# The order of side pieces in an attention stage: turned maxima first, one normalisation a step, the second half of a list later

## The chip, the cores and the metric

The kernel runs on one core of a Trainium2 chip. Its time is device time in microseconds (us) for one execution; the median of the runs is compared. The engines are TensorE (PE; its weight loads are PEld), VectorE (DVE), ScalarE (ACT), GpSimd (POOL) and SyncE (SP), which here only issues DMAs.

## What is computed

Four sequences of 512 tokens with 256 features go through two residual blocks, all in float32. The reference, cut to its core:

```python
# block 1: x = x + attn(cond_mlp(x, cond_8))
expert = jnp.argmax(opcode_onehot, axis=-1)            # one expert of 8 for a sequence
hidden = jax.nn.silu(up) * gate                        # 256 -> 512
out    = einsum('bsh,bdh->bsd', hidden, wd) + bd       # 512 -> 256
q = (einsum('bte,oe->bto', x, Wq) + bq) * scaling      # 16 heads of 16
k, v = kv[..., :16], kv[..., 16:]                      # one key and value head for all
attn_probs = softmax(einsum('brd,bsd->brs', qr, k))    # 16 x 512 query rows, 512 keys
out = einsum('bte,oe->bto', attn_output, Wo) + bo
# block 2: x = x + ffn(cond2(x, cond_8))
w_bot = einsum('bg,got->bot', y, weight * mask)        # a mixed 256 x 256 matrix per sequence
x2 = einsum('bnt,bot->bno', x, w_bot) + bias
probs = softmax(einsum('gth,he->gte', xg, w_router))   # 8 experts, 8 groups of 256 tokens
_, idx = top_k(probs, 2)                               # places by cumsum, at most 128 per group and expert
h = gelu(einsum('gech,ehf->gecf', expert_in, wi)); expert_out = einsum('gecf,efh->gech', h, wo)
out = einsum('gech,gtec->gth', expert_out, combine)
```

## The kernel before

**Stages.** First (to about 110 us) the sequences' gated layers, with the first projection. Then attention in 64 steps, with everything that a finished sequence needs next to it (output projection, mixing, routing, and the scatter of its rows to a table `xp` in DRAM that is ordered by expert). Last, from about 381 us, the expert layers: units of 256 or 128 rows of `xp` that have one expert, with 2 MB of weights for each. Every engine executes its instructions in the order in which the kernel is written: the schedule is by hand, and the lists `beside`, `last` and `final` name the side pieces of each step.

**A step.** The loop at the end of the function runs over n = 0 to 64. The step n belongs to sequence b = n // 16, with k = n % 16. It makes
- `maxima(m, ...)` for m = n + 6 (LEAD): four matmuls of scores (L375) and four reductions on VectorE (L379) that give the negated row maxima of 4 x 128 query rows in the tile `negm`;
- `exponentials(n, ...)`: four matmuls (L404) of the transposed scores of a group of 128 x 16 query rows with 128 keys, and four exponentials on ScalarE (L408);
- `weigh(n - 1, ...)`: eight products with the values (L422, 16 matmuls in the profile) into the one PSUM bank `a`; after the fourth step of a group the bank is copied to `stage` (L431: by ScalarE, in the last two groups by VectorE) and written to `od` in DRAM (L432);
- `side(b, k)`: the pieces that the lists name for this k. An entry (-1, "norm0") is piece norm0 of the sequence one back; (1, "q0") of the next; (0, ...) of the same.

The scores' matmuls write three PSUM banks `m`; the first two of each four exponentials, and the pieces, four banks `x`. In a plain step the order is: two maxima, two exponentials, half of weigh, two maxima, two exponentials, the side pieces, the other half of weigh. In a dense step, one whose pieces have large matmuls (the names in ON_PE), the pieces stand in the middle and weigh comes whole at the end. From n = 58 there are no maxima left, and a step has exponentials, weigh and side pieces.

**A group's turn.** After four steps of maxima (m % 4 == 3, so n % 4 == 1) `shifted(m // 4)` turns the group's 128 x 128 of `negm` (L387, VectorE) and writes it by four small DMAs on SP (L391) into the odd rows of the query tile. The exponentials of that group begin three steps later, and their matmuls subtract the maxima.

```python
        if m < STEPS and m % 4 == 3:
            shifted(m // 4)
```

stands at the end of the step, behind the side pieces.

**The pieces that matter here**, by their lines: `bias` adds a vector to a sequence's input rows x on VectorE (L493; x is read by `residual`, L301, into the one buffer x that the last sequence must have left); `inv` and `norm0`, `norm1` make the reciprocal of the softmax sums (L472, with a way through DRAM, L473 and L477) and multiply two halves of the attention result by it (L485); `out0` to `out3` project it (L502 on TensorE), add it to x (L507) and write the rows out (L508, SP); `rT` transposes x (L523, copied by ScalarE, L524); `mix` multiplies by the mixed matrix (L534, L538); `choose`, `rank0`, `rank1` find the two experts of each token (L551 to L582; one exponential on ScalarE between, L554); `places` counts (L600 on TensorE), `rows` and `send` compute the rows in `xp` (L613 to L649, the last being `to_i`), and `row0` to `row3` scatter (L655, eight indirect DMAs by POOL).

**The list of first units.** During the last sequence (list `last`) the first six expert units are already chosen from the first sequences' counts: `pairs0` (k = 3) starts a list of two, `pairs1` (k = 8) ends it (L840 to L876 on VectorE, fourteen small instructions) and issues on SP the fetch of the first unit's weights wi (L907; SP loads its row from the table first, L914) and of the rows xt of units 0 and 1 (L929); `pairs2` (k = 12) lists four more; `pairs3` (k = 13) fetches more weights and transposes unit 0's rows on TensorE (`turn(0)`, L971, copied by L973); `pairs4` (k = 15) fetches more weights. The rows of unit 2 are fetched first thing in the expert stage, when the scatters so far have landed, and `turn(2)` follows unit 1's first layer (L1035).

Of the kernel before, what the change touches and what calls it, by code (L numbers as in the profile page):

```python
# [42 lines left out]
def adaln_attn_ffn_kernel(  # L43
# [32 lines left out]
    def bank(tag):  # L76
        return ps.tile([P, 512], F32, tag=tag, name=f"ps_{tag}", bufs=BANKS[tag])
# [220 lines left out]
    def residual(b):  # L298

        t = rp.tile([P, 4, D], F32, name="x", bufs=1)  # L300
        nc.sync.dma_start(t, xtok[:, ts(b, 4), :])  # L301
        seqs[b]["x"] = t

    def project(b):

        s = seqs[b]
        s["q"] = q_tiles[b % 2]

        def queries(co):
            def piece():  # L310
                pq = bank("x")
                for c in range(2):
                    mm(pq, wq_sb[:, c, ts(co, P)], coT[:, c, ts(b, T)], start=c == 0, stop=c == 1)  # L313
                qs = qp.tile([P, T], F32, name="stage", bufs=4)
                nc.scalar.activation(
                    qs, pq, AF.Identity, bias=bqs_sb[:, co : co + 1], scale=HD**-0.5
                )
                for n in range(2):
                    nc.sync.dma_start(qd[co, 0:P:2, n, :], qs[ts(n, 64), :])
                nc.sync.dma_start(s["q"][:, ts(co, 2), :], qd[co])  # L320
            return piece

        def keys():

            s["k"] = qp.tile([P, T], F32, name="k")
            pk = bank("x")
            for c in range(2):
                mm(pk, wk_sb[:, c, :], coT[:, c, ts(b, T)], start=c == 0, stop=c == 1)  # L328
            nc.scalar.activation(s["k"], pk, AF.Identity, bias=bk_sb)

        def values():
            s["v"] = v_tiles[b % 2]
            pv = bank("x")
            for sc in range(4):
                nc.tensor.transpose(pv[:, ts(sc, P)], s["k"][:, ts(sc, P)], ident)
            nc.vector.tensor_copy(
                s["v"][:, :, 0:HD].rearrange("p s (j d) -> p s j d", j=2),
                pv.rearrange("p (s j d) -> p s j d", s=4, j=4)[:, :, 0:2, 3:19:2],
            )

        return {
            "q0": queries(0), "q1": queries(1), "k": keys, "v": values,
        }
# [39 lines left out]
    def shifted(u):  # L383

        b, hg = divmod(u, 4)
        nmT = qp.tile([P, 4, 32], F32, name="nmT")
        nc.vector.transpose(  # L387
            nmT.rearrange("p i t -> p (i t)"), negm[u % 2].rearrange("p i j -> p (i j)")
        )
        for a in range(4):  # L390
            nc.sync.dma_start(  # L391
                seqs[b]["q"][1:P:32, :, ds(hg * P + 32 * a, 32)],
                nmT[32 * a : 32 * a + 4],
            )

    def exponentials(n, js):
        u, sc = divmod(n, 4)
        k = seqs[u // 4]["k"]
        if n not in e_of:
            e_of[n] = ep.tile([P, 4, 4, P], F32, name="e")  # L400
        for n4, j in enumerate(js):
            px = bank("m" if n4 >= 2 else "x")
            rows_j = slice(32 * j, 32 * j + 32)
            mm(  # L404
                px, k[rows_j, ts(sc, P)], seqs[u // 4]["q"][rows_j, :, ts(u % 4, P)],
                start=True, stop=True,
            )
            nc.scalar.activation(  # L408
                e_of[n][:, :, j, :].rearrange("p h (i t) -> p i h t", i=4),
                px.rearrange("p (i h t) -> p i h t", i=4, h=4), AF.Exp,  # L410
            )
# [287 lines left out]
    def route_mixed(b):  # L699
# [25 lines left out]
        [(-1, "values"), (1, "k"), (-2, "places"), (-2, "rows")],  # L725
        [(-2, "send")],
        [(-1, "inv"), (-2, "row0")],
        [(-2, "row1")],
        [(-1, "norm0"), (-1, "norm1"), (-2, "row2")],
        [(-1, "out0"), (-1, "out1"), (-2, "row3")],  # L730
        [(-1, "out2"), (-1, "out3")],
        [(-1, "rT0"), (-1, "rT1"), (1, "v")],
        [(-1, "mix0"), (-1, "mix1")],
        [(-1, "mix2"), (-1, "mix3")],
        [],
        [(-1, "choose")],
        [(0, "bias")],
        [],
    ]
    last = [  # L740
# [1 line left out]
        [(-2, "rank1")],  # L742
        [(-1, "values"), (-2, "places"), (-2, "rows")],
        [(-1, "inv"), (0, "pairs0")],
        [(-2, "send"), (-2, "row0")],
        [(-1, "norm0"), (-1, "norm1"), (-2, "row1")],
        [(-1, "out0"), (-1, "out1"), (-1, "out2"), (-1, "out3"), (-2, "row2")],
        [(-1, "rT0"), (-1, "rT1"), (-2, "row3")],
        [(-1, "mix0"), (-1, "mix1"), (-1, "mix2"), (-1, "mix3"), (0, "pairs1")],
        [(-1, "choose"), (-1, "rank0")],  # L750
        [(-1, "rank1")],
        [(-1, "places"), (-1, "rows"), (-1, "send"), (-1, "row0")],
        [(0, "values0"), (0, "pairs2"), (-1, "row1")],
        [(0, "pairs3"), (-1, "row2")],
# [12 lines left out]
    STEPS = 16 * B  # L767
    work = {b: finish(b) for b in range(B)}

    def side(b, k):  # L770

        for off, name in (last if b == B - 1 else beside)[k]:
            to = b + off
            if not 0 <= to < B:
                continue
            if name[:5] == "pairs":
                first_pairs(name[5:])
                continue
            if off == 1:
                if name == "q0":  # L780
                    projection[to] = project(to)
                projection[to][name]()
            else:
                work[to][name]()
# [157 lines left out]
    def first_pairs(part):  # L942
        if part == "0":
            parts.append(list_of_pairs(0, N0))
            next(parts[0])
        elif part == "1":
            next(parts[0], None)
            fetch_in(0)
            fetch_rows(0)
            fetch_rows(1)  # L950
        elif part == "2":
            for _ in list_of_pairs(N0, NA - N0):
                pass
        elif part == "3":

            i = fetch_in(1)
            tc.add_manual_dep(i.ins, weighed[-1].ins.name, AFTER, reason="not at once")
            fetch_out(0)
            turn(0, "x")
        else:  # L960
            i = fetch_in(2)
            tc.add_manual_dep(i.ins, weighed[-1].ins.name, AFTER, reason="not at once")
            fetch_out(1)
# [56 lines left out]
    def up(u, half):  # L1020

        if is_small(u):
            if half == 0:
                up_small(u)
            return
        n = width(u) * P
        if half == 0:
            t = ep.tile([P, 4, 4, P], F32, name="e").rearrange("p a b t -> p (a b t)")
            hT_of[u] = t[:, 0 : F // P * n].rearrange("p (f t) -> p f t", f=F // P)
        each = 512 // n  # L1030
        for f0 in range(4 * half, 4 * half + 4, each):
            ph = bank("m")
            for k in range(each):
                for c in range(2):
                    mm(  # L1035
                        ph[:, ts(k, n)], wi_of[u][:, c, ts(f0 + k, P)], xT_of[u][:, c, :],
                        start=c == 0, stop=c == 1,
                    )
            nc.scalar.activation(  # L1039
                hT_of[u][:, f0 : f0 + each].rearrange("p f t -> p (f t)"), ph,  # L1040
                AF.Gelu_apprx_tanh,
            )
# [63 lines left out]

    for n in range(STEPS + 1):
        m = n + LEAD
        if n in (0, 26, 42, 56):
            residual((0, 26, 42, 56).index(n))  # L1110
        b, k = divmod(n, 16)
        names = [name for _, name in (last if b == B - 1 else beside)[k]] if b < B else []
        dense = any(
            name.rstrip("0123") in ON_PE and (b > 0 or name in projection[0]) for name in names
        )
        if m >= STEPS:
            if n < STEPS:
                exponentials(n, (0, 1, 2, 3))
            if n == STEPS:

                up(0, 0)
            weigh(n - 1, (2, 3))
            weigh(n - 1, (0, 1))
            if n < STEPS:
                side(b, k)
        elif dense:

            maxima(m, (0, 1))
            exponentials(n, (2, 3))
            side(b, k)  # L1130
            maxima(m, (2, 3))
            exponentials(n, (0, 1))
            if n > 0:
                weigh(n - 1, (2, 3))
                weigh(n - 1, (0, 1))
        else:

            maxima(m, (0, 1))
            exponentials(n, (2, 3))
            if n > 0:  # L1140
                weigh(n - 1, (2, 3))
            maxima(m, (2, 3))
            exponentials(n, (0, 1))
            side(b, k)
            if n > 0:
                weigh(n - 1, (0, 1))
        if m < STEPS and m % 4 == 3:
            shifted(m // 4)

    places = itertools.count()  # L1150

# [157 lines left out]
```

## Time and profile before

| | |
|---|---|
| median of 3 runs | 654.48 us (654.36 to 656.58) |
| the profiled execution | 652.61 us |
| its span, first to last instruction | 650.9 us |
| mean granted TensorE clock | 0.989 |
| TensorE busy (matmul) | 630.8 us, 97% of the span |
| VectorE, ScalarE, POOL busy | 330.4, 225.1, 111.9 us |
| L379, 250 reductions of 128x512 | 684 ns each |
| L408, 244 exponentials of 128x512 | 594 ns each |
| L493, a bias | 1.22 us |
| L387, a turn | 0.29 to 0.31 us |

The share of busy time is a mean over stages. The attention stage (about 112 to 381 us) has VectorE at half to nine tenths and DMA queues mostly idle; the expert stage has little VectorE work and DMA engines at eight to nine tenths. Matmuls are pipelined and their ends are modelled, so a TensorE that is held up for a short time can still look busy; the lengths of the steps show it better. A line of a timeline has the start, the duration, engine, line, operation, tiles and count, and in brackets how long the engine had been idle and what ended that. A row of the table of windows has a stretch, its length, the busy time of PE, PEld, DVE, ACT and POOL (with instructions), the granted clock, the share of DMA time and GB/s.

### The profile page before, as it was taken

The numbers are of one execution on the slowest core, as the hardware profiler recorded it, in microseconds if no ns is written. First come the engines' busy times: TensorE is split into PE (matmuls) and PEld (weight loads), VectorE is DVE, ScalarE is ACT, GpSimd is POOL, SyncE is SP. The second block draws the span as 40 slices with busy tenths as digits, with TensorE's granted clock in tenths as the row PEclk, the third lists the DMA queues.
The fourth block names the chain that finished last, engine by engine and source line by source line (L and its number), as shares of the span: only waits on it lengthen the run. The fifth ranks groups of instructions, "written<-read, shape, count | busy, mean of one in ns | idle before, by whom it ended". The sixth has DMA issues, their size and how long they took to land.

```text
span 650.9 us, 10666 instructions
## 1 busy us (share of the span) xinstructions
PE 630.8 (97%) x4004; PEld 373.9 (57%) x4004; DVE 330.4 (51%) x810; ACT 225.1 (35%) x400; POOL 111.9 (17%) x146
## 2 busy tenths in 40 slices
PE   9999999999999999999999899999999999999991
PEld 3444454333334433343335368888899999777781
DVE  1184745577767687867896653357122221232320
ACT  1112123566664565545554551221111112012210
POOL 1600000000000000500022141216422222312332
PEclk9999999999999999999999899999999999999996
DMA  7953981300132104411033399636899999888611
GB/s 234 360 160 90 306 250 34 98 18 34 21 130 84 51 18 117 142 58 49 19 103 116 125 318 309 210 96 207 253 268 320 322 337 298 266 259 274 193 18 23
DMA packets 65469, 107.20 MB, mean 165 GB/s; under 512 B 6915, under 2 KB 27011, under 8 KB 65411
## 3 DMA queue, kind: packets, MB, share of 16 engines
q1 hardware_dynamic: 50066, 87.96, 41.4%
q0 software_dynamic: 6464, 8.79, 6.8%
q10 hardware_dynamic: 8880, 9.71, 4.8%
q8 instruction: 33, 0.54, 0.3%
q14 instruction: 26, 0.20, 0.1%
HBM read 79.59 MB, written 26.71 MB: 163 GB/s over the span
## 4 chain that ended last, share of the span: by engine, by line
PE 87%; DMA 6%; DVE 3%; issue 1%; POOL 1%; SPq 0%; ACT 0%; POOLq 0%
PE ps_m L375 19%; PE ps_x L1068 15%; PE ps_m L1035 15%; PE ps_a L422 9%; PE ps_a L279 4%; PE ps_x L263 4%; PE ps_x L281 4%; PE ps_x L534 2%; PE ps_x L313 2%; PE ps_x L404 2%; PE ps_x L502 2%; DMA wo_sb<-in_wo_dram 2%; DMA inv<-ivd 2%; DMA inv<-od 1%; PE ps_x L1005 1%; PE ps_x L328 1%
## 5 line engine op out<-in xcount | busy, mean ns | idle before, releaser
L379 DVE TENSOR_REDUCE negm<-ps_m 128x1 f32<-128x512 f32 x250 | 160.5, 684 | 65.0 <-PE ps_x L404 46.2
L408 ACT ACTIVATE e<-ps_x 128x512 f32<-128x512 f32 x244 | 132.4, 594 | 108.5 <-PE ps_x L404 101.4
L375 PE MATMUL ps_m<-k,q 32*128 32x512 f32 x500 | 152.3, 639 | 0.4 <-DVE negm L379 0.4
L404 PE MATMUL ps_x<-q,k 32*128 32x512 f32 x488 | 139.7, 642 | 1.9 <-DMA q<-nmT 1.9
L1035 PE MATMUL ps_m<-xT,wi_sb 128*128 128x256 f32 (+1 forms) x672 | 115.4, 330 | 0.0
L1068 PE MATMUL ps_x<-wo_sb,e 128*128 128x256 f32 x512 | 114.3, 379 | 0.0
L1035 PEld LDWEIGHTS ps_m<-xT,wi_sb 128*128 128x128 f32 x672 | 103.7, 191 | 9.7 <-issue 0.4
L1068 PEld LDWEIGHTS ps_x<-wo_sb,e 128*128 128x128 f32 x512 | 95.6, 190 | 12.6 <-issue 0.4
L1039 ACT ACTIVATE e<-ps_m 128x512 f32<-128x512 f32 x64 | 38.0, 597 | 175.6 <-PE ps_m L1035 174.0
L375 PEld LDWEIGHTS ps_m<-k,q 32*128 32x128 f32 x500 | 46.5, 183 | 55.7 <-DVE negm L379 25.9
L422 PE MATMUL ps_a<-e,v 128*32 128x256 f32 x1024 | 76.6, 392 | 0.1
L1082 POOL DMA_INDIRECT out_dram<-y,to_row x36 | 55.7, 1548 | 122.2 <-DMA out_dram<-y,to_row 32.0
L422 PEld LDWEIGHTS ps_a<-e,v 128*32 128x32 f32 x1024 | 23.3, 109 | 80.2 <-issue 67.3
L973 DVE COPY xT<-ps_a 128x256 f32<-128x256 f32 (+1 forms) x23 | 12.2, 528 | 84.4 <-PE ps_a L971 84.4
L1078 DVE TENSOR_SCALAR y<-ps_x,w 128x256 f32<-128x256 f32 x32 | 15.4, 482 | 63.9 <-PE ps_x L1068 63.9
L655 POOL DMA_INDIRECT xp<-x,to_i x32 | 33.6, 1051 | 53.8 <-DVE negm L379 28.8
L404 PEld LDWEIGHTS ps_x<-q,k 32*128 32x128 f32 x488 | 38.2, 184 | 4.4 <-issue 4.2
L584 POOL TENSOR_SCALAR x<-mk 128x4 f32<-128x4 f32 x4 | 0.8, 211 | 208.2 <-DVE mk L581 208.1
L284 DVE SCALAR_TENSOR_TENSOR hid<-ps_x,wo_sb,sg 128x512 f32<-128x512 f32 x16 | 12.0, 749 | 45.2 <-PE ps_x L281 45.2
L279 PE MATMUL ps_a<-xT_sb,wi_sb 128*128 128x512 f32 x64 | 30.5, 599 | 0.1
L281 PE MATMUL ps_x<-xT_sb,wi_sb 128*128 128x512 f32 x64 | 30.1, 592 | 0.0
L263 PE MATMUL ps_x<-hid,wo_sb 128*128 128x512 f32 x64 | 28.8, 597 | 0.0
(165 smaller groups left out, 464.7 us busy)
## 6 DMA issues: line engine op xcount, KB each, us to landing
wi_sb<-in_wi_dram SPq DMA_DIRECT2D x25, 1024.0 KB
wo_sb<-in_wo_dram SPq DMA_DIRECT2D x25, 1024.0 KB
xp<-zeros ACTq DMA_DIRECT2D x1, 8712.0 KB
q<-qd SPq DMA_DIRECT2D x8, 512.0 KB
wi_sb<-in_wcond_dram SPq DMA_DIRECT2D x15, 256.0 KB
od<-stage SPq DMA_DIRECT2D x15, 256.0 KB
xt<-xp SPq DMA_DIRECT2D x11, 264.0 KB
wo_sb<-in_wcond_dram SPq DMA_DIRECT2D x4, 517.0 KB
```

The source lines that it names most:

```text
L263: mm(po, wd[:, hc, ts(dc, P)], hid_of[b][:, hc, :], start=hc == 0, stop=hc == 3)
L279: mm(pu, wu[:, c, :], xT_sb[:, c, ts(b, T)], start=c == 0, stop=c == 1)
L281: mm(pg, wg[:, c, :], xT_sb[:, c, ts(b, T)], start=c == 0, stop=c == 1)
L375: mm(pm, q[32 * j : 32 * j + 32, i, ts(hg, P)], k[32 * j : 32 * j + 32, :], start=True, stop=True,)
L379: nc.vector.tensor_reduce(nm[:, i, j : j + 1], pm, AX.X, ALU.max, negate=True)
L404: mm(px, k[rows_j, ts(sc, P)], seqs[u // 4]["q"][rows_j, :, ts(u % 4, P)], start=True, stop=True,)
L408: nc.scalar.activation(e_of[n][:, :, j, :].rearrange("p h (i t) -> p i h t", i=4), px.rearrange("p (i h t) -> p i h t", i=4, h=4), AF.Exp,)
L422: i = mm(pa_of[u][32 * hh : 32 * hh + 32, j0 * P : (j0 + nj) * P], seqs[b]["v"][:, sc, :], e[:, hh, j0 : j0 + nj].rearrange("p j n -> p (j ...
L1035: mm(ph[:, ts(k, n)], wi_of[u][:, c, ts(f0 + k, P)], xT_of[u][:, c, :], start=c == 0, stop=c == 1,)
L1039: nc.scalar.activation(hT_of[u][:, f0 : f0 + each].rearrange("p f t -> p (f t)"), ph, AF.Gelu_apprx_tanh,)
L1068: mm(po[:, 0:D], hT_of[u][:, fc, ts(h, P)], wo_of[u][:, fc, :], start=fc == 0, stop=fc == F // P - 1,)
L1082: i = nc.gpsimd.indirect_dma_start(out=out_rows, out_offset=bass.IndirectOffsetOnAxis(ap=to, axis=0), in_=y, in_offset=None, compute_op=AL ...
```

## The change

`shifted` moves from the end of the step to the place behind the last exponentials: in a plain step ahead of the side pieces, in a dense one ahead of weigh. In `beside` (sequences 0 to 2) the bias of a sequence moves from k = 14 of its own steps to k = 5 of the next sequence's; `norm0` and `norm1` are parted to k = 6 and 7; the output pieces, transposes, mixes and the values of the next sequence (`v`) move one step back, to k = 8 to 12; `choose` stays at 13. In `last` (the steps of sequence 3) the bias of sequence 2 comes at k = 4, ahead of the send of sequence 1; `pairs1` moves from k = 8 to k = 10, behind the second rank, where no maxima are left; the last sequence's own bias stays at k = 14. The reading of x for sequences 1 and 2 moves from n = 26 and 42 to 27 and 43. The number of instructions stays the same.

```diff
     beside = [
...
         [(-1, "inv"), (-2, "row0")],
-        [(-2, "row1")],
-        [(-1, "norm0"), (-1, "norm1"), (-2, "row2")],
-        [(-1, "out0"), (-1, "out1"), (-2, "row3")],
+        [(-1, "bias"), (-2, "row1")],
+        [(-1, "norm0"), (-2, "row2")],
+        [(-1, "norm1"), (-2, "row3")],
+        [(-1, "out0"), (-1, "out1")],
         [(-1, "out2"), (-1, "out3")],
         [(-1, "rT0"), (-1, "rT1"), (1, "v")],
         [(-1, "mix0"), (-1, "mix1")],
         [(-1, "mix2"), (-1, "mix3")],
+        [(-1, "choose")],
         [],
-        [(-1, "choose")],
-        [(0, "bias")],
         [],
     ]
     last = [
...
         [(-1, "inv"), (0, "pairs0")],
-        [(-2, "send"), (-2, "row0")],
+        [(-1, "bias"), (-2, "send"), (-2, "row0")],
...
-        [(-1, "mix0"), (-1, "mix1"), (-1, "mix2"), (-1, "mix3"), (0, "pairs1")],
+        [(-1, "mix0"), (-1, "mix1"), (-1, "mix2"), (-1, "mix3")],
         [(-1, "choose"), (-1, "rank0")],
-        [(-1, "rank1")],
+        [(-1, "rank1"), (0, "pairs1")],
...
-        if n in (0, 26, 42, 56):
-            residual((0, 26, 42, 56).index(n))
+        if n in (0, 27, 43, 56):
+            residual((0, 27, 43, 56).index(n))
...
             side(b, k)
             maxima(m, (2, 3))
             exponentials(n, (0, 1))
+            if m % 4 == 3:
+                shifted(m // 4)
...
             maxima(m, (2, 3))
             exponentials(n, (0, 1))
+            if m % 4 == 3:
+                shifted(m // 4)
             side(b, k)
...
-        if m < STEPS and m % 4 == 3:
-            shifted(m // 4)
```

## The prediction, made before the changed kernel was run

> **What bounds the kernel now.** I read the page, then a table of windows cut at the ends of the steps, then the end of the attention stage engine by engine.
>
> The page, parts 1 and 2: TensorE works nearly all the time, so only stretches in which it waits can be won, and one slice of the clock row (the 23rd, 358 to 374 us) is below full speed.
> ```profile
> PE 630.8 (97%) x4004; PEld 373.9 (57%) x4004; DVE 330.4 (51%) x810; ACT 225.1 (35%) x400; POOL 111.9 (17%) x146
> PEclk9999999999999999999999899999999999999996
> ```
> Windows; a row is a stretch, its length, each engine's busy time, granted clock, DMA share:
> ```profile
> 221.71:226.83 5.12, 5.12 (x44) 2.48 (x44) 3.35 (x7) 2.17 (x5) 0.00 (x0) 1.00 0.19 70
> 226.83:230.36 3.53, 3.53 (x36) 1.19 (x36) 2.36 (x5) 1.77 (x5) 0.00 (x0) 1.00 0.00 0
> 237.44:241.52 4.08, 4.08 (x37) 1.34 (x36) 4.08 (x6) 2.18 (x6) 0.00 (x0) 1.00 0.01 1
> 200.31:206.52 6.21, 5.61 (x44) 2.64 (x44) 5.37 (x10) 2.58 (x6) 0.00 (x0) 1.00 0.20 69
> 272.38:279.11 6.73, 5.48 (x44) 2.50 (x44) 5.38 (x9) 2.56 (x6) 3.18 (x3) 1.00 0.45 161
> 357.38:362.15 4.77, 4.39 (x36) 1.23 (x35) 3.71 (x10) 2.22 (x5) 0.00 (x0) 1.00 0.64 195
> 367.11:373.09 5.98, 4.07 (x32) 1.45 (x32) 2.88 (x18) 2.44 (x6) 1.05 (x1) 0.75 0.02 4
> ```
> In order: a step with matmuls of side pieces (5.12); a plain one (3.53); the one after a bias (4.08, VectorE busy throughout); the ones after a pair of normalisations, sequences 1 and 2 (6.21, 6.73, against 5.12); step 57, behind the list's second half (4.77); step 60, which waits and then runs at 0.75 clock. Its cause, in the timeline of TensorE, VectorE and SP:
> ```profile
> 357.86 0.42 SPq L907 DMA_DIRECT2D wi_sb<-in_wi_dram  x1
> 361.60 1.29 DVE L379 TENSOR_REDUCE negm<-ps_m 128x1 f32<-128x512 f32 x2 [0.94 <-PE ps_x L404]
> 365.16 0.30 DVE L387 STREAM_TRANSPOSE nmT<-negm 128x128 f32<-128x128 f32 x1
> 367.31 0.39 PE L600 MATMUL ps_x<-hot,ones 128*128 128x64 f32 x2
> 369.61 0.74 PE L404 MATMUL ps_x<-q,k 32*128 32x512 f32 x2 [1.91 <-DMA q<-nmT]
> 370.86 0.17 DVE L649 TENSOR_TENSOR to_i<-pos,to 128x8 int32<-128x8 f32 x1
> 373.16 0.69 DVE L431 COPY stage<-ps_a 128x512 f32<-128x512 f32 x1 [2.13 <-PE ps_a L422]
> 375.33 0.66 PE L971 MATMUL ps_x<-ident,xt 128*128 128x128 f32 x4
> 387.94 0.38 SPq L929 DMA_DIRECT2D xt<-xp  x1
> 396.11 0.57 PEld L971 LDWEIGHTS ps_a<-ident,xt 128*128 128x128 f32 x4
> ```
> The last maxima are reduced at 362.89, but turned only at 365.46, behind the router's choice; TensorE gets them 4.15 later.
>
> **Part A, pieces in steps 0 to 56.** A bias keeps VectorE for 1.14 us (237.94 to the next reduction at 239.08), and the step after it is 0.55 longer: 0.59 of a piece is absorbed. Before: three biases, 0.64, 0.54, 0.55 (steps of 4.18, 4.07, 4.08); two pairs of normalisations, 6.21 − 5.12 = 1.09 and 6.73 − 5.12 = 1.61; together 4.43. After, in sequences 1 and 2: the bias stands behind the turn (0.31) of the same step, 1.14 + 0.31 − 0.59 = 0.86; the first normalisation (0.95, half of the pair's 1.89) 0.95 − 0.59 = 0.36; the second ends 0.95 after its reductions, while TensorE wants it for out0's second product some 0.75 after them, 0.2: 1.42, twice 2.84. The last sequence's step 4 gets a bias ahead of the send; there VectorE runs without a break from 316.85 (DVE-bound steps of 3.7 to 4.6), so the bias costs its whole 1.14. The turn ahead of both its normalisations delays them by 0.3, which the 0.31 idle found before 337.24 pays. After 3.98, gain **0.45**. Ends: with nothing absorbed beyond the 0.45 that VectorE idles per half step, seven pieces cost 0.14 more each, a loss of 0.5; with normalisations free, a gain of 1.55. I take the middle rows, as the bias is the nearest piece.
> The four output pieces, the two transposes and the mixes move a step later, with their out_dram DMAs on SP and copies on ACT; five such steps stay five, and SP waits there for adds that are due anyway: 0, and 0.3 an output piece (its add is 0.42) if not. Reading x at 27 and 43 moves with the transposes; its reader is ten steps off. The turns of k 1 and 13 change places with a piece of their own step: 0, at most the 0.31 of one turn.
>
> **Part B, the list's second half leaves step 56.** VectorE is freed of 355.70 to 358.15 (2.45); step 57 becomes plain, 4.77 − 3.54: gain 1.23. On SP the weight fetch and two row fetches (357.86 to 360.97) go behind the four turn DMAs.
>
> **Part C, the last turn.** Reductions now end at 362.89 − 1.23 = 361.66, the turn at 361.97, its data reaches TensorE 4.15 later, 366.12. TensorE comes at 367.69 (end of L600) − 1.23 = 366.46: the wait goes. Step 60 lasts 2.31 (the plain tail step 373.09 to 375.40) and not 373.09 − 367.69 = 5.40: gain 3.09, of it 1.91 waiting and 1.18 half clock. B and C promise 4.32.
>
> **Part D, what is late next.** VectorE's queue behind the turn: choice and first rank 2.43 (362.81 to 365.24), second rank 1.26, now the list 2.45, then rows and send 3.31 (367.73 to 371.04), and only then L431's copy (0.69), which empties the one bank that step 61's weighing writes: 361.97 + 2.43 + 1.26 + 2.45 + 3.31 + 0.69 = 372.11. TensorE is there at 366.46 + 2.31 + 1.31 (the exponentials' products) = 370.08: it waits 2.1. Weighing ends at 373.17; then it wants turn(0)'s rows. The trace's DMA records have them landed at 364.21, 8.51 after the list began; the list now begins at 365.66, so 374.17: another 1.0. The transposes end at 374.83, before at 375.99: of 4.32, **1.16** is left.
> Then turn(2), at 396.11. Its rows (issued 387.94, when the last of eight scatters had landed) are complete at 396.00 in the DMA records: TensorE had 0.1 us to spare. They hang on to_i, at 371.04 before and 371.42 after, and on queue q1, which serves wi and xt until 374.5 and then the rest, which in before began at 374.71. So they land no earlier, TensorE waits some 1.05 there, and **0.1** is kept. Ends: 1.16 kept, if the landing moves with TensorE; a loss of 0.3, if it follows to_i.
> The waits of 2.1 and 1.0 may bring the half clock back. The trace: after 1.91 us without work the clock was 0.75 over step 60, costing 1.18; by that row the same again is lost, and the 1.05 of waiting at turn(2) takes it in but for 0.1.
> [...]
>
> **The sum.** 0.45 + 0.1 − 0.1 ≈ 0.45. The profiled execution took 652.61 (span 650.9 and 1.7 around it): 652.15 after. The runs' median, 654.48, lies 1.9 above it; the same change gives **654.0**. A measurement of this kernel tells about 0.5% (3.3 us) from no change.
>
> **Rivals.**
> *Kept as far as turn(0)* (19%): landings move with TensorE. For it: scatters and fetches follow the same step. Against: their source, to_i, does not move. 654.48 − 0.45 − 1.16 = 652.9.
> *All kept* (13%): if choice, ranks and list leave the copy and turn(0) no later than TensorE wants them. For it: VectorE is 49% idle over the span. Against: the 10.1 us of queue counted in D. 654.48 − 0.45 − 4.32 = 649.7; with half of D's waits, 651.5.
> *The fetches push the DMA queue* (11%): the moved fetch's packets (358.95 to 364.53, 5.58 us, in a stretch otherwise idle) now end where the crowded stretch starts; a window from 374 to 640 us has a DMA share of 0.80. If they delay all behind them by X, turn(2) passes on all but 0.1. From X = 0.6 it is slower than before, from X = 3.9 by over 0.5%; with all 5.58: 654.48 − 0.45 + 5.58 − 0.1 = 659.5. Against: the sum has them done 0.2 before that stretch.
> *VectorE's pieces cost more* (7%): A at its bad end, no half clock hidden: 654.48 + 0.5 + 1.1 = 656.1.
> The forecast itself has 50%, with 653.2 to 655.0. Faster by over 0.5% (below 651.2) is most of *all kept*, 12%; slower (above 657.8) most of the queue's, 10%; within, 78%. The range, 651.8 (A's best end and 1.16 kept) to 656.4 (A's bad end, 0.3 lost at turn(2), and a half clock not hidden), leaves out some 2 in 10.
>
> **What would show it.** Step 57 at 3.5; no wait for q<-nmT at step 60; TensorE waiting at L422 for the copy of L431, then at L971 for xt; the copy straight after to_i; a half clock around 372 to 377; turn(2) with a wait. Steps of about 4.4 after the bias, of 3.9 and 5.3 with the normalisations, 1.1 more at the last sequence's step 5. Wrong would be a tail in which VectorE has idle time before L431, or rows of turn(2) that come a microsecond earlier.

## The result, and the profile after

| | changed | before |
|---|---|---|
| median of 12 runs each, side by side | 654.04 | 655.14 |
| lowest to highest | 652.75 to 656.07 | 653.78 to 656.63 |
| profiled execution (span) | 653.83 (652.0) | 652.61 (650.9) |
| step 56 ends at | 357.69 | 357.38 |
| step 64 ends at | 386.75 | 385.53 |

The ratio is 0.9993, with a 95% interval of 0.9981 to 1.0006: no difference that can be measured. The quotient of the two medians, 0.9983, lies in that interval too. The profiled execution of the changed kernel is typical of its runs; that of the kernel before was 2.5 below the median of the 23 runs that came with the first experiments (655.15). A second profile of the kernel before, told below, took 654.56.

Three lines of the page of the changed kernel, of busy times, clock and costliest groups:

```profile
PE 633.2 (97%) x4004; PEld 375.6 (58%) x4004; DVE 331.1 (51%) x810; ACT 225.0 (35%) x400; POOL 111.4 (17%) x146
...
PEclk9999999999999999999999989999999999999997
...
L422 PE MATMUL ps_a<-e,v 128*32 128x256 f32 x1024 | 76.6, 392 | 1.4 <-DVE cmp L823 1.3
```

TensorE's busy time grew by 2.4 (630.8 before) with as many matmuls: some of them ran at half clock, in a later slice than before. And L422 now has idle time in front of it, 1.4, released by VectorE.

Windows cut at the ends of steps 22, 23, 24, 53, 55, 57, 61 and 62, with the columns as in the prediction:

```profile
196.41:200.91 4.50, 4.50 (x37) 1.44 (x36) 4.45 (x8) 2.18 (x6) 0.00 (x0) 1.00 0.52 173
200.91:204.45 3.54, 3.54 (x34) 1.20 (x34) 3.19 (x6) 2.17 (x6) 0.00 (x0) 1.00 0.02 4
204.45:209.72 5.27, 5.27 (x44) 2.68 (x44) 4.26 (x8) 2.56 (x6) 0.00 (x0) 1.00 0.16 53
332.86:337.69 4.83, 4.46 (x37) 1.22 (x36) 4.68 (x12) 2.65 (x7) 1.04 (x1) 1.00 0.47 165
345.38:350.79 5.41, 5.41 (x45) 2.47 (x44) 3.85 (x6) 4.22 (x8) 1.96 (x2) 1.00 0.42 130
357.69:361.23 3.54, 3.54 (x37) 1.20 (x36) 2.41 (x5) 2.26 (x6) 0.00 (x0) 1.00 0.20 74
...
368.90:373.14 4.24, 2.90 (x25) 1.03 (x24) 3.79 (x22) 3.21 (x7) 0.94 (x1) 1.00 0.92 320
373.14:379.29 6.15, 5.00 (x31) 1.90 (x31) 3.82 (x15) 1.19 (x2) 4.79 (x5) 0.50 0.89 256
```

The reader is to see: the step behind a bias (4.50), behind the first normalisation (3.54, as if nothing were there) and behind the second (5.27); the bias in the last sequence (4.83); step 57 without the list (3.54). Then what came instead: step 61, with 1.34 without a matmul, and step 62, all of it at a clock of 0.50.

The timeline of the end, lines of VectorE and TensorE:

```profile
361.74 0.31 DVE L387 STREAM_TRANSPOSE nmT<-negm 128x128 f32<-128x128 f32 x1
...
371.15 0.17 DVE L649 TENSOR_TENSOR to_i<-pos,to 128x8 int32<-128x8 f32 x1
...
371.24 0.68 DVE L431 COPY stage<-ps_a 128x512 f32<-128x512 f32 x1
...
372.07 1.07 PE L422 MATMUL ps_a<-e,v 128*32 128x256 f32 x16 [1.34 <-DVE cmp L823]
...
374.29 1.12 PE L971 MATMUL ps_x<-ident,xt 128*128 128x128 f32 x4 [1.15 <-DMA xt<-xp]
...
397.53 0.60 PE L971 MATMUL ps_a<-ident,xt 128*128 128x128 f32 x4
```

The last turn comes 3.42 earlier than before (365.16), and no wait for q is left. L422 starts right behind the copy L431, which stands in VectorE's queue behind the choice, the list and the send (the profile names the small instruction that ends 0.05 before it). Then TensorE waits for the first unit's rows. The clock was half from 373.18 to 380.01, 6.83, against 3.41 before.

### The profile page after: what moved, and what is told of

It reads as the page before. It is cut to its first block, busy times and chain, and to the rows that moved or that the text cites. A ratio compares the mean times of both kernels' runs of the same rounds, so it can differ in the third digit from the quotient of the medians.

```text
span 652.0 us, 10666 instructions
## 1 busy us (share of the span) xinstructions
PE 633.2 (97%) x4004; PEld 375.6 (58%) x4004; DVE 331.1 (51%) x810; ACT 225.0 (35%) x400; POOL 111.4 (17%) x146
## 4 chain that ended last, share of the span: by engine, by line
PE 92%; DVE 3%; DMA 2%; issue 1%; POOL 1%; SPq 0%; ACT 0%; POOLq 0%; DVEq 0%
PE ps_m L375 20%; PE ps_m L1035 17%; PE ps_x L1068 16%; PE ps_a L422 10%; PE ps_a L279 4%; PE ps_x L263 4%; PE ps_x L281 4%; PE ps_x L534 2%; PE ps_x L313 2%; PE ps_x L502 2%; PE ps_x L404 2%; PE ps_a L971 1%; PE ps_x L1005 1%; PE ps_x L328 1%; PE ps_m L985 1%; DVE negm L379 1%
## 5 line engine op out<-in xcount | busy, mean ns | idle before, releaser
L422 PE MATMUL ps_a<-e,v 128*32 128x256 f32 x1024 | 76.6, 392 | 1.4 <-DVE cmp L823 1.3
L422 PEld LDWEIGHTS ps_a<-e,v 128*32 128x32 f32 x1024 | 23.4, 109 | 81.5 <-issue 65.2
L655 POOL DMA_INDIRECT xp<-x,to_i x32 | 33.1, 1035 | 58.3 <-DVE negm L379 29.7
```

Source lines behind the costliest of these rows:

```text
L422: i = mm(pa_of[u][32 * hh : 32 * hh + 32, j0 * P : (j0 + nj) * P], seqs[b]["v"][:, sc, :], e[:, hh, j0 : j0 + nj].rearrange("p j n -> p (j ...
```

## The experiments

"Before" in each ratio is the kernel before on the same chip; the times in brackets are lowest to highest.

### Four first: one part alone, and the list earlier

`list_alone` moves only `pairs1`:

```diff
-        [(-1, "mix0"), (-1, "mix1"), (-1, "mix2"), (-1, "mix3"), (0, "pairs1")],
+        [(-1, "mix0"), (-1, "mix1"), (-1, "mix2"), (-1, "mix3")],
...
-        [(-1, "rank1")],
+        [(-1, "rank1"), (0, "pairs1")],
```

> The list's second half is moved to step 58, nothing else is changed. Theory (what the move of the list frees at step 57, 1.2 us, is given back in VectorE's queue at the copy of L431 and at the rows of turn(0)): step 57 plain, 3.54; the wait for q<-nmT at step 60 stays near 1.9 us; turn(0) ends about 1.2 us earlier than before, and turn(2) takes most of that: ratio to before 0.998 to 1.000. Rival (the fetch that moves with it crowds the DMA queue): 1.003 or more.

Measured: 654.40 (652.64 to 657.92), ratio 1.0 (0.9981 to 1.0019). Step 57 took 3.54; the wait for q was still there, 1.23 instead of 1.91, with 3.41 of half clock behind it; TensorE then waited 0.47 at L971. The list's 1.23 is won at step 57 and given back in the tail, in this profile above all in step 63 (4.65 against 2.65).

`turn_alone` moves only the calls of `shifted`:

```diff
             exponentials(n, (0, 1))
+            if m % 4 == 3:
+                shifted(m // 4)
             side(b, k)
...
-        if m < STEPS and m % 4 == 3:
-            shifted(m // 4)
```

> Only the turn goes ahead of the side pieces; the list stays at step 56. Theory: the q<-nmT wait of 1.9 us and its half clock go, the rows of turn(0) are there early, and the copy of L431 makes TensorE wait 0.5 us at most, so turn(0) ends 2.5 us earlier than before; some of it is lost at turn(2): ratio 0.996 to 0.998, better than the whole change. Rival (the wait just goes on to the next late thing, whatever the list does): 0.999 to 1.000.

Measured: 658.77 (658.12 to 661.05), ratio 1.0058 (1.0042 to 1.0074): slower, against the expectation. The wait for q went as foreseen (step 60 took 2.66), but step 63 took 7.89 and step 64 6.45. That was the surprise of this study; the next group of runs is about it.

`pieces_alone` has the lists of the changed kernel, but the turn and `pairs1` as before:

```diff
-        [(-2, "row1")],
-        [(-1, "norm0"), (-1, "norm1"), (-2, "row2")],
-        [(-1, "out0"), (-1, "out1"), (-2, "row3")],
+        [(-1, "bias"), (-2, "row1")],
+        [(-1, "norm0"), (-2, "row2")],
+        [(-1, "norm1"), (-2, "row3")],
+        [(-1, "out0"), (-1, "out1")],
...
-        [(0, "bias")],
+        [],
...
-        [(-2, "send"), (-2, "row0")],
+        [(-1, "bias"), (-2, "send"), (-2, "row0")],
```

> Only the bias, normalisations, outputs, transposes and mixes are moved; turn and list stay. The prediction had a gain of 0.45 us (ratio 0.9993); the profiles of before and after, step by step up to step 56, have a loss of 0.45 us (1.0007), most of it at the last sequence's steps 53 to 55 (1.8 us). Theory: 1.000 to 1.001. Rival (the loss in steps 53 to 55 is only how one profile was recorded): 0.999.

Measured: 653.14 (652.19 to 653.47), ratio 0.9959 (0.9946 to 0.9972): faster than expected. In its profile it still waits for q (1.60), but the clock stays full to the end of the attention stage (1.00 from 366 to 390), as in the profiles of both later kernels that were made from this one. Where the gain comes from, the profiles do not show: the profiled execution was the slowest of the five runs, and its span (651.8) lies between those of the two profiles of the kernel before (650.9 and 652.9).

`early_list` is the changed kernel with the list's second half at k = 7 and its fetches at k = 8 of the last sequence:

```diff
-        [(-1, "rT0"), (-1, "rT1"), (-2, "row3")],
-        [(-1, "mix0"), (-1, "mix1"), (-1, "mix2"), (-1, "mix3")],
+        [(-1, "rT0"), (-1, "rT1"), (-2, "row3"), (0, "pairs1")],
+        [(-1, "mix0"), (-1, "mix1"), (-1, "mix2"), (-1, "mix3"), (0, "pairsf")],
...
-        [(-1, "rank1"), (0, "pairs1")],
+        [(-1, "rank1")],
...
             next(parts[0], None)
+        elif part == "f":
             fetch_in(0)
```

> The changed kernel, with the list's second half on VectorE in step 55 and its fetches (SP alone) in step 56, so that VectorE's queue behind the last turn is 2.45 us shorter and the rows of turn(0) land some 10 us earlier. Theory: no wait at L422 (1.34 in the changed kernel) nor at L971 (1.15), no half clock there, so turn(0) ends 2.5 to 3 us earlier than in the changed kernel; turn(2) takes a part: ratio to before 0.994 to 0.997. Rival (turn(2)'s rows set the end whatever happens before them): 0.998 to 1.000.

Measured: 656.16 (654.76 to 656.97), ratio 1.0005 (0.9995 to 1.0014). Both waits of the prediction's part D were gone, as expected; but step 56, right behind the list's new place, took 8.10 instead of 6.90, step 63 took 8.20 and step 64 5.71, as long as with the turn alone (7.89 and 6.45). So a third thing stands behind the two waits.

### What holds step 63

In the timeline of `turn_alone` (ScalarE, GpSimd and TensorE), the exponentials of step 62:

```profile
378.34 0.60 ACT L408 ACTIVATE e<-ps_x 128x512 f32<-128x512 f32 x1 [3.34 <-PE ps_a L422]
...
379.14 1.05 POOL L655 DMA_INDIRECT xp<-x,to_i  x1 [0.30 <-issue]
...
379.73 0.60 ACT L408 ACTIVATE e<-ps_x 128x512 f32<-128x512 f32 x1 [0.80 <-PE ps_m L404]
...
381.17 1.09 ACT L408 ACTIVATE e<-ps_m 128x512 f32<-128x512 f32 x2 [0.84 <-remote]
...
381.82 1.73 PE L404 MATMUL ps_m<-q,k 32*128 32x512 f32 x2 [2.44 <-ACT e L408]
```

The four products that these exponentials read ended together at 376.5. ScalarE takes them at 378.34, 379.73 and 381.17, some 1.4 apart, though one exponential takes 0.60; TensorE then waits 2.44 for a bank that ScalarE has not read. ScalarE was not busy: what came late was the word that the products were done. The trace records when each semaphore was raised: here at 378.25, 379.71 and 381.15, each just ahead of one of the three starts. For every matmul that raises one I took the first raise after its end (matmul ends are modelled, so a single number is rough) and counted those over 0.5 late; "in the scatters" means between the first of a sequence's eight scatters (L655) and 4 us behind the last:

```
profile             late  in the scatters  half clock, 360 to 400  step 64 ends  execution
before                 3                3                    3.41        385.53     652.61
before_again          27               27                    3.41        387.43     654.56
after                 18               18                    6.83        386.75     653.83
list_alone            27               27                    3.41        385.92     653.03
turn_alone            26               25                    6.83        391.87     658.62
pieces_alone          23               22                    0           386.35     653.47
early_list            23               22                    6.83        389.55     656.31
turn_early_values     32               29                    3.41        387.58     654.37
after_early_values    24               23                    6.83        389.98     656.71
pieces_list           19               18                    0           385.66     652.45
pieces_bias14         25               24                    0           386.37     653.04
after_act_copy        28               24                    0           385.93     652.78
```

Nearly all late raises lie in the four stretches in which GpSimd issues eight scatters, whatever the kernel. The first profile of the kernel before is the exception, with three, and none between 366 and 400; it is also the one that ran 2.5 below its median. The counts are upper bounds: that profile has all of its 869 raises, the others miss 5 to 21, mostly in the same stretches, and where one is missing its matmul can count as late. In the end of the attention stage of `turn_alone` (368 to 388) none is missing.

A window of half clock, in the expectations, is 3.41 of it, as in the profile of the kernel before; two are the 6.83 of `turn_alone`. The half clock also shows in the mean granted clock, which is on record for every run: in the profiles of the table it is 0.991 to 0.993 with no half clock in this stretch, 0.989 or 0.990 with 3.41 and 0.988 with 6.83. It parts the twelve runs of `early_list`: seven at 0.987 or 0.988 took 656.06 to 656.97, five at 0.990 took 654.76 to 655.18. It does not part those of the changed kernel: six at 0.987 or 0.988 took 652.87 to 655.07, six at 0.989 to 0.991 took 652.75 to 656.07.

In the stretch of `turn_alone` shown above SP also loads the last sequence's sums and values. `turn_early_values` is `turn_alone` with these loads three steps earlier, and `after_early_values` the changed kernel with the same edit:

```diff
-        [(-1, "choose"), (-1, "rank0")],
+        [(0, "values0"), (-1, "choose"), (-1, "rank0")],
...
-        [(0, "values0"), (0, "pairs2"), (-1, "row1")],
+        [(0, "pairs2"), (-1, "row1")],
```

> The run with the turn alone lost its gain at step 63: semaphore posts of TensorE came 1.4 us apart from 374.1 on and ScalarE, idle 3.34 us, got the exponentials' products late. In that stretch SP loads the last sequence's sums and values (four transfers in rows of 2048 bytes, issued 374.12 to 375.39) while GpSimd scatters sequence 2's rows. Here these loads are issued at step 57 instead of 60, when the queues are idle. Theory (the loads on top of the scatters make the hold-up): no gap above 1 us at L404 in step 63, at most one window of half clock, ratio 0.994 to 0.999. Rival (the scatters alone, or something else, make it): the gap of 2.4 us and two windows of half clock stay, ratio 1.004 to 1.007.

> The changed kernel with the same loads at step 57. The waits for the copy (1.3) and for the rows of the first unit (1.15) stay under both theories, for the loads have nothing to do with VectorE's queue. Theory: step 62 falls from 6.15 to under 4.5, ratio 0.994 to 0.998. Rival (scatters, or the two waits themselves, make the long step 62): step 62 stays at 5 to 6, ratio 0.998 to 1.001 as for the changed kernel.

Measured: 656.91 (654.37 to 657.86), ratio 1.0041 (1.0027 to 1.0054), and 654.94 (652.89 to 656.71), ratio 1.0002 (0.999 to 1.0013). In the profile of the first, the fastest of its five runs, the late raises stayed; step 63 took 5.86 instead of 7.89 and the half clock lasted 3.41 instead of 6.83. So the loads do not make the raises late; whether they make the hold-up longer is open. In the second the profile, the slowest of its twelve runs, shows another price: TensorE waited 4.21 for the first unit's rows, which were issued behind the loads and the weights, and step 62 took 9.03.

`turn_late_rows` is `turn_alone` with the eight scatters of sequence 2 issued behind step 64, and `after_late_rows` the changed kernel with the same edit:

```diff
-        [(-1, "places"), (-1, "rows"), (-1, "send"), (-1, "row0")],
-        [(0, "values0"), (0, "pairs2"), (-1, "row1")],
-        [(0, "pairs3"), (-1, "row2")],
-        [(0, "bias"), (-1, "row3")],
+        [(-1, "places"), (-1, "rows"), (-1, "send")],
+        [(0, "values0"), (0, "pairs2")],
+        [(0, "pairs3")],
+        [(0, "bias")],
...
+    for ch in range(4):
+        work[B - 2][f"row{ch}"]()
     places = itertools.count()
```

> In every profile so far the semaphore posts of TensorE that come over 0.5 us behind the end of their matmuls lie in the four stretches in which GpSimd issues eight scatters of rows (264 to 276, 337 to 349, 372 to 384, 438 to 450 us). Here, with the turn alone moved, the eight scatters of sequence 2 are issued behind step 64. The rows of the third unit are then read later and TensorE waits for them behind 396, so only steps 60 to 64 are read. Theory (the scatters hold up the posts): no post over 0.5 us late between 366 and 384, step 63 at 3.3 or less instead of 7.89, step 64 at 4.65 instead of 6.45, full clock throughout; step 64 ends 5 us or more earlier than with the turn alone. Rival (the weight fetches, or something bound to the step, hold them up): step 63 at 5 or more.

> The changed kernel with the same eight scatters behind step 64. The waits at L422 for the copy (1.3) and at L971 for the rows of the first unit (1.1) have nothing to do with the scatters and stay. Theory (the rest of step 62 was the hold-up): step 62 falls from 6.15 to between 3.8 and 5.0 (the upper end with one window of half clock), step 64 ends 1 to 2.5 us earlier than in the changed kernel. Rival (the two waits and the half clock they bring make all of step 62): step 62 stays within 0.4 of 6.15.

Measured, one run each: 660.16 and 663.88, with TensorE waiting for the third unit's rows behind step 64, as said beforehand. Windows of steps 63 and 64, first of `turn_alone`:

```profile
377.53:385.42 7.89, 5.46 (x25) 1.48 (x25) 1.81 (x2) 4.34 (x8) 4.99 (x6) 0.80 0.95 320
385.42:391.87 6.45, 6.45 (x33) 4.67 (x34) 0.00 (x0) 2.37 (x3) 0.00 (x0) 0.72 1.02 358
```

and of `turn_late_rows`:

```profile
376.86:379.69 2.83, 2.83 (x26) 1.30 (x25) 1.35 (x2) 2.82 (x7) 0.00 (x0) 1.00 0.85 237
379.69:384.34 4.65, 4.65 (x33) 3.37 (x34) 0.00 (x0) 2.76 (x4) 0.00 (x0) 1.00 1.04 381
```

The loads and weight fetches are there in both (DMA share 0.85 and more); GpSimd's column falls from 4.99 to 0 in the first row, and 6.86 us go: no late raise between 366 and 384, and full clock. Late raises turned up at 391.8 and 395.3, where the scatters now are. So in this stretch the late raises go with the scatters: shown, by one profile each. The scatters do not bring them in every execution (the first profile of the kernel before has none here), and how they do it was not looked into: GpSimd's work and the DMA traffic of the scatters were moved together.

In `after_late_rows` the theory held only in part: step 62 took 5.09 instead of 6.15, just above the 3.8 to 5.0 that were expected, but step 61 took 5.10 instead of 4.24, and steps 57 to 64 took 28.30 against 29.06, 0.76 less and not 1 to 2.5. The wait for the copy (1.34) stayed, the one for the first unit's rows was 0.38 instead of 1.15, and the 6.83 of half clock stayed. So in the profile of the changed kernel the waits and the clock, and not the scatters, make most of the loss.

### The wait for the copy, by itself

`after_act_copy` is the changed kernel with the copy of the second last group on ScalarE, as in the groups before it:

```diff
-            (nc.vector.tensor_copy if u >= 4 * B - 2 else nc.scalar.copy)(o, pa_of[u])
+            (nc.vector.tensor_copy if u >= 4 * B - 1 else nc.scalar.copy)(o, pa_of[u])
```

> The changed kernel with the copy of the second last group's result (L431) on ScalarE, which takes it out of VectorE's queue behind the choice, the list and the send. Theory (the two waits of the prediction stand in series before the same rows, which land at the same time): the wait of 1.34 at L422 goes, that at L971 grows from 1.15 to 2 or more, step 64 ends within 0.5 of the changed kernel, ratio 0.998 to 1.001. Rival (the copy is what TensorE waits for, and the half clock comes from it): the wait goes, the clock stays full, step 64 ends 2 to 4 us earlier, ratio 0.993 to 0.996.

Measured: 652.38 (651.67 to 653.18), ratio 0.9959 (0.9946 to 0.9972). Timeline, and windows of steps 61 and 62:

```profile
370.05 0.62 ACT L431 COPY stage<-ps_a 128x512 f32<-128x512 f32 x1
...
374.51 0.63 PE L971 MATMUL ps_x<-ident,xt 128*128 128x128 f32 x4 [2.63 <-DMA xt<-xp]
```
```profile
369.05:371.87 2.82, 2.82 (x24) 0.94 (x24) 2.48 (x17) 2.82 (x7) 0.00 (x0) 1.00 0.83 285
371.87:377.20 5.33, 2.69 (x32) 1.22 (x31) 4.61 (x19) 1.69 (x4) 3.94 (x4) 1.00 0.89 315
```

Each theory was half right. ScalarE makes the copy 1.19 earlier than VectorE did, the wait at L422 is gone, and the one at L971 grew from 1.15 to 2.63, since the rows land when they did (374.51 against 374.29): the sum of the waits is nearly the same, 2.63 against 2.49. But the clock stayed full in this profile. Steps 61 to 64 took 16.88 against 17.84, although step 64 lost 1.25 here, in a stretch with late raises (5.90 against 4.65): from 0.96 and 1.25, an estimate of some 2.2 for the half clock in the profile of the changed kernel. This version, with five runs, is faster than both kernels; its interval lies outside that of the changed kernel (0.9981 to 1.0006). That the full clock makes it faster is not shown: by the marks of the mean granted clock three of its five runs (0.990) had some half clock too, and they took 651.67 to 652.38, less than the profiled run with full clock (652.78, at 0.993).

### The pieces again, and a second look at the kernel before

`pieces_list` is `pieces_alone` with `pairs1` moved as in `list_alone`; `pieces_bias14` is `pieces_alone` with the bias of sequence 2 in its own step 14:

```diff
-        [(-1, "bias"), (-2, "send"), (-2, "row0")],
+        [(-2, "send"), (-2, "row0")],
...
     def side(b, k):
+        if (b, k) == (B - 2, 14):
+            work[b]["bias"]()
```

> Pieces as in the changed kernel and the list's second half moved, but the turn left where it was. The pieces alone gave 0.9959, the list alone 1.0. Theory (what the list's move frees is given back at the tail, whatever stands before it): 0.9945 to 0.997, not told from the pieces alone. Rival (the three parts add up, and the turn is what costs): 0.994 or less, some 1.2 us under the pieces alone.

> The pieces of the changed kernel without its turn and list, which gave 0.9959, and with the bias of sequence 2 back in that sequence's own step 14 instead of the last sequence's step 4. The prediction's price for that place was the whole 1.14, against 0.55 to 0.64 in a step of its own. Theory: step 53 falls from 4.83 to 3.7, step 47 rises from 3.54 to 4.1; together 0.6 won, ratio 0.993 to 0.997. Rival (what the pieces win has nothing to do with these steps and their tail is a matter of chance): the two steps change as said, but the ratio is 0.998 to 1.001.

Measured: 652.41 (651.81 to 656.90), ratio 0.9985 (0.9966 to 1.0003), and 653.04 (651.99 to 654.04), ratio 0.9968 (0.9957 to 0.998). The first has the lower median, but 4 of its 12 runs took 654 to 657 (the three slowest at a granted clock of 0.988, where six at 0.992 or 0.993 took 651.81 to 652.45), and its gain over the pieces alone is not told from nothing. In the second, steps 47 and 53:

```profile
309.05:313.02 3.97, 3.97 (x36) 1.22 (x36) 3.96 (x6) 2.17 (x6) 0.00 (x0) 1.00 0.01 1
333.30:337.00 3.70, 3.66 (x37) 1.23 (x36) 3.26 (x11) 2.65 (x7) 1.04 (x1) 1.00 0.55 182
```

3.97 instead of 3.54, and 3.70 instead of 4.83: the bias costs 0.43 in its own step (priced at 0.55 to 0.64) and 1.13 in the last sequence's (1.14). The 0.7 does not show in the time (653.04 against 653.14).

> A second profile of the kernel before, whose first profile (652.61) lay 2.5 us below the median of its runs (655.15). If the spread comes from the stretch of 372 to 390 us, the time up to step 59 agrees with the first profile within 0.3 us, and a time nearer 655 shows a gap in steps 61 to 64 or a second window of half clock that the first has not. Rival: the spread comes from the experts' stage behind 390 us, and the end of step 64 agrees within 0.5 us.

Measured: 654.56. Step 59 ended 0.82 later than in the first profile, outside the 0.3 of the theory; step 64 ended 1.90 later, and all behind it took 254.64 against 254.58 from the third unit's transposes on. So the spread lies ahead of the end of step 64, 0.82 of it in the steps up to 59 and 1.08 in the tail, and not in the experts' stage. The step in which it waits for q:

```profile
367.93:374.27 6.34, 4.33 (x32) 1.66 (x31) 2.88 (x18) 2.18 (x6) 1.24 (x2) 0.73 0.02 4
```

It is 0.36 longer than in the first profile (5.98), with nearly the same wait (2.01) and the same half clock (3.41); the rest of the tail's loss comes in steps 62 and 63 (0.50 and 0.38), where the late raises are (376 to 383).

## Why the prediction was right, and where not

The forecast was 654.0 against 654.48, a ratio of 0.9993, and 0.9993 was measured. The waits that it named are in the profile, step by step. That the number fits so well is in part luck: two terms of the tail were wrong in opposite directions, and the parts alone did not do what the sum says. The pieces, priced at a gain of 0.45, gave 0.9959, some 2.7; the turn, whose gain (3.09) the tail was to take back, gave 1.0058, a loss of some 3.8; the list 1.0. Their product, 1.0017, is not told from 0.9993 within their intervals.

- **Part A.** Behind bias and turn the steps took 0.96 and 0.86 more (0.86 predicted), behind the second normalisation 0.17 each (0.2), in the last sequence 1.14 (1.14). Behind the first normalisation nothing (0.36): VectorE was busy 3.19 of 3.54, so its piece fitted. With the prediction's 4.43 for before, that makes a gain of 1.13 where 0.45 stood. Not foreseen: steps 16, 32 and 49 grew by 0.42, 0.21 and 0.21, and step 55 by 0.92. The last lies in a stretch of scatters with late raises (344 to 349), and took 4.50 in `after_act_copy`, which has the same order there, and 5.66 in the second profile of the kernel before; so it belongs to the execution. With step 54 (0.21 shorter) the sum is a loss of some 0.4 in this pair of profiles, a gain of some 0.5 without step 55. Both are within the ends that the part gave. One term of before was of its execution too: the step of 6.73 took 6.08 in the second profile. And the 2.7 of the pieces alone lies outside those ends; the profiles do not account for it.
- **Part B.** Right: 4.77 to 3.54.
- **Part C.** Right: no wait for q. Steps 59 and 60 together fell from 8.62 to 5.60, 3.02 against 3.09 predicted.
- **Part D, the first two waits.** Right in place and order: the copy straight behind to_i ended at 371.92 (372.11 predicted), and TensorE took up the rows at 374.29 (374.17). The wait at L422 was 1.34 and not 2.1 (2.03 by the prediction's own figures), as steps 59 and 60 took 2.94 and 2.66 and not the 2.64 and 2.31 taken from the kernel before; the wait at L971 was 1.15 (1.0). `after_act_copy` confirms that the rows, and not the copy, set the end of the two.
- **Part D, the third unit.** This step failed. "They land no earlier, TensorE waits some 1.05 there, and 0.1 is kept" did not happen: in every profile with the scatters in place the third unit's transposes start 10.78 to 10.80 behind the end of step 64, which is the work between them, without a wait. In the changed kernel step 64 ended 1.22 later than before, and the rows landed 0.58 earlier (by the last raise of their fetch's semaphore: 395.42 against 396.00), 2.1 ahead of their use at 397.53. The landing does not go with the end of step 64: it came at 396.00 with an end at 385.53 (before), at 393.30 with 385.66 (`pieces_list`) and at 393.99 with 389.55 (`early_list`). No version with the scatters in place ended step 64 earlier than the first profile's 385.53, so how much could be kept there was not seen.
- **Part D, the half clock.** Foreseen as possible, but mis-sized: priced at 1.18 with all but 0.1 hidden at the third unit. In the profile it lasted 6.83, cost some 2.2 by the estimate above, and nothing hid it, since there was no wait to hide it in. In this pair of profiles the changed kernel won 4.50 in steps 57 to 60 (4.32 predicted) and lost 5.40 in steps 61 to 64: 2.49 in the two waits, some 2.2 by the clock, the rest not accounted for. So the tail took the gain back, but not by the way that the prediction gave. How much of it the clock takes in the other runs is open: those of the changed kernel with a higher granted clock were not faster.
- **The base.** The terms were taken from an execution nearly free of late raises. The second profile of the same kernel has 27 of them and took 1.95 more, which is more than the change was worth; that the late raises are all of this spread was not shown.
- **The rivals.** The queue pushed by the fetches: no, everything from the third unit's transposes on took 254.51 against 254.58 (from 396.32 in before). All kept: its condition (nothing late next) did not hold. Kept as far as turn(0): not tried, as step 64 ended no earlier than before. The pieces cost more, with no half clock hidden: the pair of profiles looks like it (1.22 slower, where it had 1.6), the runs do not, as its ratio of 1.0025 lies outside the measured interval.

At the end of the attention stage half clock lasted 3.41 in the profile of the kernel before, with a wait of 1.91, and 6.83 in that of the changed kernel, with waits of 1.34 and 1.15; in `after_act_copy` it did not come with one of 2.63.

## What to carry to other kernels

A wait that goes at the end of a stage is worth only what the next late thing leaves (in the profiles here 4.50 were won in steps 57 to 60 and 5.40 lost in steps 61 to 64): list what stands in the queues behind it, to the first transfer whose landing does not move, and look for the copy that holds a bank, which another engine may make (ScalarE made it 1.19 earlier in `after_act_copy`). Whether the clock falls could not be told here from the lengths of the waits (half for 6.83 with 1.34 and 1.15, full with 2.63); read the granted clock of every run, and not of the profiled one alone, before a gain or a loss is put down to it. And take the base of a sum from more than one profiled execution when the gain is under half a per cent: two profiles of one kernel differed here by 1.95, more than the change was worth.

## What was not expected of the hardware

- While GpSimd issued scatters by index (L655 in the changed kernel: mostly 0.98 to 1.05 each, one every 1.29), raises of TensorE's semaphores came late, by 0.58 to 3.60 in the profile of the changed kernel (18 raises), and in the turn alone ScalarE took finished products 1.4 apart (378.34, 379.73, 381.17), where two exponentials without a wait between them took 1.08 (372.93). Steps 63 and 64 of the turn alone, with their half clock, were 6.86 longer than with the scatters moved behind step 64, and the late raises moved with the scatters. Why is open, and so is why one profile of the kernel before has nearly none (3, of 0.61 to 0.63).
- After nearly the same sum of waits (2.49 and 2.63) the clock was half for 6.83 in one kernel and full in the other. In the four profiles whose clock stayed full (`pieces_alone`, `pieces_list`, `pieces_bias14`, `after_act_copy`) the longest wait of TensorE at the end of the attention stage was 1.59 to 2.63; with half clock it was, for one, 1.23 in `list_alone` (3.41 of it) and 4.21 in `after_early_values` (6.83). What decides it was not settled; the same kernel can differ by it from run to run, as the granted clocks show (0.987 to 0.991 in the changed kernel).
